# Four stacked graph-attention layers on one core: three pair sums kept in SBUF, and more steps for roots, source scores and turned rows

## The chip, the cores and the metric

The kernel runs on 1 core of one Trainium2 chip. The metric is the device time of one execution in microseconds. Engines are named as in the profile: PE is TensorE (matmul) and PEld its weight loads, DVE is VectorE, ACT is ScalarE, POOL is GpSimd, SP is SyncE, which here issues nearly all DMAs.

## The reference

A graph of N = 3327 nodes with 256 features each, a dense 0/1 adjacency matrix, and four attention layers, each followed by a residual sum and a layer norm. The last layer holds three attention steps of its own.

```python
def _L0(features, adj, Wq, Wk):                  # cosine attention
    att = where(adj > 0, Kn @ Qn.T, NEG); att = softmax(att, axis=1)
    prop = adj_mask * (att @ features) + (1 - adj_mask) * features
    return 0.5 * prop + 0.5 * features
def _L1(x, adj, W, a):                           # graph attention with leaky relu
    h = x @ W
    e = leaky_relu((h @ a[:D]) + (h @ a[D:]).T, 0.01)
    return elu(softmax(where(adj > 0, e, MASK_VAL), axis=1) @ h)
def _L2(x, adj, Wq, bq, Wk, bk, Wv, bv):         # dot-product attention
    q, k, v = x @ Wq.T + bq, x @ Wk.T + bk, x @ Wv.T + bv
    return elu(softmax(where(adj > 0, q @ k.T / sqrt(256), neg), axis=-1) @ v)
def _L3(x, adj, W0, W1, a1, W2, a2, W3, a3):     # x @ W0, then three steps like _L1
x = layernorm(x + _Li(x, adj, ...))              # for i = 0, 1, 2, 3
```

## The kernel before, in words

**Tiles and blocks.** The nodes are padded to 3328: NT = 26 tiles of 128 source nodes, and NB = 7 blocks of target nodes, six of 512 (4 tiles) and a last one of 256 (2 tiles). A pass (`Layer`, with keys 0, 1, 2, 3a, 3b, 3c) runs over the blocks b, and a block over the 26 steps j. A step makes one tile of attention weights (128 source nodes by 512 target nodes) and multiplies it into the values of these 128 nodes: the product goes to PSUM (`po`), where the block's sums gather.

**Weights.** In layers 0 and 2 PE makes scores (`ps`, L459 and L523), ACT takes the exponential (`ex`, L468 and L531), and DVE multiplies by the mask (`e`, L448). In layers 1, 3a, 3b and 3c ACT makes them from a row of source scores `u` and a column (`re`, L617), and DVE multiplies by the mask (`e`, L628). `make` runs LA = 2 steps ahead of the products.

**Products.** Most blocks multiply `e` straight into the values (L1282). Layer 2 and blocks 1 to 5 of layer 0 take two steps together in seven products instead of eight (`products`, L738). For this DVE adds and subtracts weights (`ssum`, L686 to L689), and four sums of the values of tiles 2p and 2p+1 are wanted (`tsums`, 128 x 513 floats for a pair p of 13). `combine` makes them once on DVE (L662 to L671) and writes them to DRAM (`t_d`, L672); `fetch_tsum` (L676) reads a pair back when a block comes to it. Tiles of the tag `tsum` have 3 buffers. For layer 0 `combine` is called in block 0, for pairs 0 to 12 at steps 9 to 21. In layer 2 the last pair's sums are used from SBUF in block 0 without a fetch.

**Adjacency.** In layer 0 each block's adjacency comes in 13 pieces of two tiles (`stage`, 512 KB, 3 buffers, L400). ACT turns a piece into a byte mask (L411, L412), and DVE adds it to a sum (`acc`, L416 and L420). At the end of a block `sum_adj` copies the sum (`af`, L431), and PE turns it (`pasum`, L435). The mask is written to DRAM (L890) for the later passes, which fetch it for a block (L385).

**Ends of blocks.** `finish` is a generator: it divides by the sums, applies the layer's weight, activation and norm, and stops at each `yield`. One part of it runs at each step of the next block (`advance`), and at j = 20 what is left is run at once. It holds: the copy of `po` (`p`, L916, or `y`, L872), which frees PSUM; `turn` (ACT copies `planes`, L793, a transposing DMA `turned`, L796, some steps of waiting, DVE copies, L803) for the rows before the projection (`pT`, then `pproj`, L947) and, in layer 1, for the normed rows (`ft`, then `pv`, L1032, then `combine` for layer 2); the dot products for the next pass's scores (`sd`, L551); after the last whole block, b = NB - 2 = 5, their greatest values and exponentials (`shift`, `keys`); and `rows`, where PE turns the source scores (`psr`, L595), ACT copies them (`srow`) and SP writes them (`s_d`). In the last block the mean row (`pmean`, L819) closes the values.

**Queries.** In layer 0 `queries0` prepares the next block's queries by such steps too: squares on ACT (L350), reciprocal roots on POOL (`rk`, L135 to L148), after some steps the scaling on ACT (`kr`, L366), the turning on PE (`pkT`, L370) and a copy on ACT (L371).

**Order.** Only the first four steps of the program stand in the order written. After that the tile framework's scheduler orders each engine's instructions from its own costs; the order in which the generators record them is what it starts from. [...] Tiles of one tag share a few buffers: `x4k` has two (for `xT`, `gT`, `y4`, layer 2's `tsum`, `planes`, `pT4`), PSUM's `pb` three, `po` five.

## Time and profile before

| what | value |
|---|---|
| runs of the kernel before | 2383.55, 2384.17, 2386.76 us (median 2384.17) |
| the profiled execution | 2385.32 us, of it 2383.5 us from the first to the last instruction |
| PE busy | 2349.8 us |
| PE's clock | 0.995 of full speed on average; 0.50 from 12.95 to 16.37 us and from 98.29 to 105.11 us |
| layer 0, block 0 | to 106 us |
| layer 0, blocks 1 to 6 | to 484 us |
| layer 1 | to 836 us |
| layer 2 | to 1408 us |
| passes 3a, 3b, 3c | to about 1727 us, 2047 us and the end |

The profile is of one execution. Times in it count from its first instruction. "Idle before" is the time an engine did nothing ahead of an instruction, with what ended it behind the arrow; in the chain, "issue" is time in which an engine waited for nothing that the profile shows. The ends of matmuls are modelled, so a wait of PE is best read from starts.

### The profile page before, as it was taken

Reading aid. Unit: us, or ns where it says so; the run is one execution under the profiler, and the core shown is the slowest. Engines: PE = TensorE matmul, PEld = TensorE weight load, DVE = VectorE, ACT = ScalarE, POOL = GpSimd, SP = SyncE. Lnnn points to the kernel's source line nnn. Section 1 sums busy time; section 2 is a strip of 40 time slices with the busy share of each in tenths; the row PEclk is TensorE's granted clock in tenths of the full one; section 3 lists DMA queues with packets and bytes.
Section 4 is the critical chain, followed back from the end, with each engine's and each line's share of the span. In section 5 each row is a group of like instructions: output and inputs, shape, how many; then the busy total and the mean of one; then the engine's idle time right before and its main releaser. Section 6 shows DMA issues by size and latency. Waiting matters only on the chain.

```text
span 2383.5 us, 33176 instructions
## 1 busy us (share of the span) xinstructions
PE 2349.8 (99%) x11965; PEld 1916.8 (80%) x11965; DVE 1609.4 (68%) x4318; ACT 1222.2 (51%) x1959; POOL 42.1 (2%) x168
## 2 busy tenths in 40 slices
PE   9999999999999999999999999999999999999997
PEld 6677787888888777667767798888888888888886
DVE  6779999966676657567567585556656555655665
ACT  4667776765555422222222255565655555655554
POOL 0000000000000000000000000000000000000000
PEclk9999999999999999999999999999999999999998
DMA  8555555523222322212212221221211111132120
GB/s 262 183 166 180 193 188 179 172 81 95 74 69 70 100 56 87 69 63 87 70 53 73 78 91 47 64 60 29 71 51 43 43 59 48 46 97 69 60 66 22
DMA packets 147720, 215.45 MB, mean 90 GB/s; under 512 B 76141, under 2 KB 101220, under 8 KB 142948
## 3 DMA queue, kind: packets, MB, share of 16 engines
q1 hardware_dynamic: 147284, 213.07, 28.9%
q8 instruction: 94, 1.54, 0.3%
q14 instruction: 70, 0.57, 0.1%
q10 hardware_dynamic: 272, 0.26, 0.0%
HBM read 168.32 MB, written 28.19 MB: 82 GB/s over the span
## 4 chain that ended last, share of the span: by engine, by line
PE 88%; DVE 7%; ACT 2%; DMA 2%; issue 1%; POOL 0%; POOLq 0%; SPq 0%; DVEq 0%; ACTq 0%
PE po L1282 48%; PE po L738 16%; PE ps L523 12%; PE ps L459 4%; PE pproj L947 3%; DVE e L448 1%; PE pv L1032 1%; PE pgq L482 1%; DVE acc L420 1%; DVE ejunk L551 1%; DMA turned<-planes 1%; PE po L1267 1%; ACT re L617 1%; DMA stage<-in_adj_a 1%; PE pq L305 1%
## 5 line engine op out<-in xcount | busy, mean ns | idle before, releaser
L1282 PE MATMUL po<-v,e 128*128 128x257 f32 x5616 | 1252.2, 381 | 1.9 <-ACT p L916 1.4
L1282 PEld LDWEIGHTS po<-v,e 128*128 128x128 f32 x5616 | 1063.2, 190 | 169.3 <-issue 10.9
L617 ACT ACTIVATE re<-u,nrh,th 128x512 f32<-128x512 f32 (+1 forms) x728 | 556.2, 780 | 478.4 <-DVE e L628 474.2
L628 DVE SCALAR_TENSOR_TENSOR e<-re,rh,mask 128x512 f32<-128x512 f32 (+1 forms) x702 | 502.5, 719 | 379.2 <-PE po L1282 355.8
L448 DVE SCALAR_TENSOR_TENSOR e<-ex,mask 128x512 f32<-128x512 f32 (+1 forms) x364 | 235.3, 649 | 198.9 <-ACT ex L531 157.8
L523 PE MATMUL ps<-gT,ft 128*128 128x512 f32 (+1 forms) x728 | 307.4, 563 | 0.0
L531 ACT ACTIVATE ex<-ps,off 128x512 f32<-128x512 f32 (+1 forms) x182 | 119.2, 656 | 359.9 <-PE ps L523 333.3
L738 PE MATMUL po<-tsums,ssum 128*128 128x128 f32 (+1 forms) x1794 | 250.9, 275 | 1.4 <-DVE ssum L688 1.2
L738 PEld LDWEIGHTS po<-tsums,ssum 128*128 128x128 f32 x1794 | 224.8, 192 | 3.3 <-DVE ssum L688 2.7
L523 PEld LDWEIGHTS ps<-gT,ft 128*128 128x128 f32 x728 | 132.1, 190 | 114.5 <-issue 111.7
L738 PEld LDWEIGHTS po<-v,e 128*128 128x128 f32 x1196 | 169.2, 191 | 68.0 <-issue 51.2
L738 PE MATMUL po<-v,e 128*128 128x129 f32 x1196 | 182.9, 275 | 1.9 <-DVE e L448 1.8
L468 ACT ACTIVATE ex<-ps,rq 128x512 f32<-128x512 f32 (+1 forms) x182 | 118.0, 653 | 115.9 <-PE ps L459 103.9
L459 PE MATMUL ps<-ft,ft 128*128 128x512 f32 (+1 forms) x312 | 143.4, 565 | 0.9 <-ACT ex L468 0.9
L420 DVE CUSTOM_DVE_ANT_0 acc<-acc,stage 128x1024 uint16<-128x1024 uint16 (+1 forms) x168 | 108.5, 646 | 14.7 <-DMA stage<-in_adj_a 10.9
L738 PE MATMUL po<-v,ssum 128*128 128x128 f32 x598 | 92.3, 275 | 0.0
L738 PE MATMUL po<-tsums,e 128*128 128x128 f32 x598 | 92.1, 275 | 0.0
L412 ACT ACTIVATE mask<-pos 128x1024 uint8<-128x1024 bf16 (+1 forms) x87 | 86.3, 992 | 2.0
L411 ACT ACTIVATE pos<-stage 128x1024 bf16<-128x1024 int32 (+1 forms) x87 | 85.6, 983 | 0.0
L947 PE MATMUL pproj<-w_l_w,pT 128*128 128x256 f32 x304 | 78.0, 381 | 3.5 <-DVE pT L803 3.5
L738 PEld LDWEIGHTS po<-v,ssum 128*128 128x128 f32 x598 | 79.4, 192 | 0.1
L738 PEld LDWEIGHTS po<-tsums,e 128*128 128x128 f32 x598 | 79.3, 192 | 0.0
(245 smaller groups left out, 1739.5 us busy)
## 6 DMA issues: line engine op xcount, KB each, us to landing
mask<-mask_d SPq DMA_DIRECT2D x30, 1664.0 KB
stage<-in_adj_a SPq DMA_DIRECT2D x78, 512.0 KB
tsums<-t_d SPq DMA_DIRECT2D x155, 256.5 KB
mask_d<-mask SPq DMA_DIRECT2D x6, 1664.0 KB
u<-s_d SPq DMA_DIRECT2D x24, 256.0 KB
xT<-in_xT SPq DMA_DIRECT2D x10, 512.0 KB
mask<-mask_d SPq DMA_DIRECT2D x5, 832.0 KB
t_d<-tsums SPq DMA_DIRECT2D x14, 256.5 KB
```

Source lines behind the costliest of these rows:

```text
L412: nc.scalar.activation(mask(b, j, 2), t_[:, : 2 * wd], AF.Sign)
L420: nc.vector.tensor_tensor(acc, acc, st[:, h * wd : (h + 1) * wd], ALU.add)
L448: nc.vector.scalar_tensor_tensor(e[:, :wd], t_[:, :wd], 0.0, mask(b, j), ALU.add, ALU.mult)
L459: nc.tensor.matmul(ps[:, :wd], FT[j // 4][:, 0, (j % 4) * P : (j % 4 + 1) * P], FT[b][:, 1, :wd], start=True, stop=True,)
L468: nc.scalar.activation(t_[:, :wd], ps[:, :wd], AF.Exp, scale=rq[:, j : j + 1])
L523: nc.tensor.matmul(ps[:, :wd], FT[j // 4][:, h, (j % 4) * P : (j % 4 + 1) * P], g[:, h, :wd], start=(h == 0), stop=(h == 1),)
L531: nc.scalar.activation(t_[:, :wd], ps[:, :wd], AF.Exp, bias=off, scale=1.0 / D**0.5)
L617: nc.scalar.activation(t_[:, :wd], self.u[b][:, :wd], AF.Relu, bias=self.nrh[:, j : j + 1], scale=self.th[:, j : j + 1],)
L628: nc.vector.scalar_tensor_tensor(e[:, :wd], t_[:, :wd], self.rh[:, j : j + 1], mask(b, j), ALU.add, ALU.mult,)
L738: nc.tensor.matmul(o, x, y, start=(p == 0 and g not in banks[:i]), stop=(p == NT // 2 - 1 and g not in banks[i + 1 :]),)
L947: nc.tensor.matmul(pm[:, :D], pT[:, h, :], w[L.w][:, h, :], start=(h == 0), stop=(h == 1),)
L1282: nc.tensor.matmul(pos[k], es[:, k * P : (k + 1) * P], V[L.i % 2][j], start=(j == 0), stop=(j == NT - 1),)
```

## The change

Five things change: which pair sums are fetched, and when some parts are recorded. What is computed stays the same.

1. The first three pairs' sums of layer 0 are kept for block 1: `combine` makes pairs 3 to 11 at steps 9 to 17, pair 12 at step 20 and pairs 0, 1, 2 at steps 21, 22, 23, and `make` doesn't fetch pairs 0 to 2 in block 1. They are still written to DRAM for the later blocks.
2. `queries0` waits 7 steps instead of 4 after the roots on POOL, except for block 1's queries.
3. After layer 0's last whole block two more steps stand ahead of `rows`.
4. `turn` waits longer for `pT` in the last block (5 steps in layer 1, 6 in 3a and 3b, instead of 3) and after the last whole block of 3a, 3b and 3c (6 instead of 5), and for layer 1's normed rows after the last whole block (4 instead of 3).
5. The end of layer 1's last whole block may run over steps 0 to 25 of the next block instead of 0 to 20.

```diff
@@ queries0
-            for _ in range(4):
+            for _ in range(4 if g == 1 else 7):
                 yield
@@
+    kept = {("0", 0): 1, ("0", 1): 1, ("0", 2): 1, ("2", NT // 2 - 1): 0}
+
     def combine(key, p, v, e=None):
...
-        here = key == "2" and p == NT // 2 - 1
-        if here or key == "0":
+        if (key, p) in kept or key == "0":
             t = work.tile([P, 4 * H + 1], F32, tag="tsum", name="tsums", bufs=3)
         else:
             t = work.tile([P, 4 * H + 1], F32, tag="x4k", name="tsum", bufs=2)
-        if here:
-            tsums[0, p] = t
+        if (key, p) in kept:
+            tsums[kept[key, p], p] = t
@@ finish, the rows for pT
-                    5 if b == NB - 2 else 3,
+                    3 if b < NB - 2 else 5 if L.key == "1" else 6,
@@ finish, layer 1's normed rows
+                    4 if b == NB - 2 else 3,
@@ finish, ahead of rows, b == NB - 2
                 L.gat_next.keys(0, ts_[-1] + 1)
                 yield
+                if L.key == "0":
+                    yield
+                    yield
@@ make
-        if strassen(L, b) and j % 2 == 0 and (L.key, b, j) != ("2", 0, NT - 2):
+        if strassen(L, b) and j % 2 == 0 and kept.get((L.key, j // 2)) != b:
             fetch_tsum(L.key, b, j // 2)
@@ the steps
-        if first and 0 <= j - 9 < NT // 2:
-            combine("0", j - 9, V[0], es)
+        if first and 9 <= j < 18:
+            combine("0", j - 6, V[0], es)
+        elif first and 20 <= j < 24:
+            combine("0", (j - 21) % (NT // 2), V[0], es)
@@
-        if j == 20 and not end:
+        if j == (25 if L.key == "1" and b == NB - 1 else 20) and not end:
             while pending:
                 advance()
```

## The prediction

> **What bounds the kernel now.** I read the busy times of the page first, then the chain, then PE's own idle stretches in the trace, and last what ended each of them.

> ```profile
> PE 2349.8 (99%) x11965; PEld 1916.8 (80%) x11965; DVE 1609.4 (68%) x4318; ACT 1222.2 (51%) x1959; POOL 42.1 (2%) x168
> ...
> PE 88%; DVE 7%; ACT 2%; DMA 2%; issue 1%; POOL 0%; POOLq 0%; SPq 0%; DVEq 0%; ACTq 0%
> ```

> PE works 99% of the span, and the diff neither adds nor removes a matmul. So only PE's idle time, 33.7 us of 2383.5, and time at a lowered clock can change. Idle stretches over 0.15 us come to 20.2 us in 21 places. The largest is the end of block 0 of layer 0 (timeline, columns: start, length, engine and line, then in brackets the idle time before and what ended it):

> ```profile
> 92.87 0.32 SPq L676 DMA_DIRECT2D tsums<-t_d  x1
> 93.28 0.38 SPq L400 DMA_DIRECT2D stage<-in_adj_a  x1
> ...
> 97.90 1.42 DVE L420 CUSTOM_DVE_ANT_0 acc<-acc,stage 128x1024 uint16<-128x1024 uint16 x2 [3.24 <-DMA stage<-in_adj_a]
> 99.24 0.68 DVE L448 SCALAR_TENSOR_TENSOR e<-ex,mask 128x512 f32<-128x512 f32 x1
> 99.84 0.42 DVE L431 CAST af<-acc 128x512 f32<-128x512 int32 x1
> ...
> 100.40 1.08 PE L435 MATMUL pasum<-ident,af 128*128 128x128 f32 x4 [4.44 <-DVE af L431]
> ```

> The adjacency piece is issued only at 93.28, behind a fetch of pair sums; DVE waits 3.24 us for it, in order, ahead of the last weights and of af; PE stands 4.44 us. The table by windows shows a second price, the granted clock (last but two columns):

> ```profile
> 94.88:98.29 3.41, 1.08 (x5) 0.59 (x4) 0.39 (x1) 1.35 (x2) 0.00 (x0) 1.00 1.04 336
> 98.29:105.11 6.82, 4.71 (x11) 3.25 (x12) 4.09 (x10) 0.69 (x1) 0.00 (x0) 0.50 0.56 237
> 408.87:412.28 3.41, 1.57 (x6) 0.90 (x6) 2.90 (x12) 3.38 (x5) 0.00 (x0) 1.00 0.11 42
> ```

> After a window with PE busy 1.08 of 3.41 us (32%) the clock is 0.50 for 6.82 us, and 4.71 us of matmuls run in it: 2.35 us lost. A window with 46% busy (408.87) lost no clock. The other places that the diff aims at:

> ```profile
>   POOL rk L148: 22.3, 6
> ```

> (what the instructions on tile kr waited for: ACT stands 22.3 us for roots on POOL; the trace shows PE losing 3.1 us of it at 408 to 414 and 0.8 us at 141 to 147, nothing in the other blocks), and three pieces of the chain:

> ```profile
> 466.92 0.27 PE psr L595
> ...
> 822.74 1.37 DVE ft L803 x2
> ...
> 824.24 3.69 PE pv L1032 x16
> ...
> 1708.53 0.72 DVE pT L803
> ```

> PE stands 1.15 us before psr, 0.96 before pv (for turned rows), 0.57 at 1708.7 and 0.66 at 2028.4 for pT.

> [...]the piece at 93.28 had its buffer free since ACT's L411 ended at 89.14.

> **The change part by part.** A scheduler sets each engine's order from the recorded steps, so I compared the built orders of the two kernels, engine by engine; a part whose orders don't move can't act.

> *Kept pair sums.* Three fetches (L676) leave SP at the end of block 0. Sums of pairs 3 to 11 are now made at steps 9 to 17, pair 12 at 20, pairs 0 to 2 at 21 to 23; the 13 writes stay. DVE does the same 65 small operations; 5 of them with the roots between take about 2.1 us (86.4 to 88.4), without roots 1.4. New order on SP: piece, write, piece (1,0), write of 12, piece (1,2), writes of 0 and 1, piece (1,4), write of 2.
> Step by step, with old durations: piece (1,0) waited for the write at 80.08 and left at 80.50; its buffer was free at 78.5 (L411 of 77.44 plus 1.05), so it leaves 2 us earlier and DVE's 0.46 us wait for it goes. Piece (1,2) left at 86.34 behind a fetch; now at 83.55 (L411 ends 83.51), landing by about 88. DVE, with two sums fewer before it, does the first sum of (1,0) at 82.9, weights, pair 0 with roots (to 86.2), weights, pair 1 with roots (to 88.4), half of (1,2) to 89.0, the last operation of pair 1 at 89.3. That releases its write (89.35) and piece (1,4) at 89.75, against 93.28. From issue to DVE's start took 4.62 us (93.28 to 97.90) behind a transfer of the same size issued 0.4 us before it; I keep that: 94.4. From there to pasum is 2.50 us as before: 96.9 instead of 100.40, **3.5 us**. Pair 2's sums (1.4 us) go into DVE's wait. PE is done with v_24's first matmul at 95.3 (the 0.47 us wait at 93.1 is gone), so it stands 1.6 us: a window stays at least 53% busy, above the 46% that kept the clock: **2.35 us** more. Bounds: if (1,4) takes 5.8 us (as from 86.34 to 92.16) 2.3 us and no clock; if the wait vanishes 5.1 + 2.35. I take 5.85.
> Behind the later write on SP stand the mask's 1.66 MB (now about 92.7, before 93.72) and piece (1,6), first used after 103: free. Pair 3's fetch still waits for pair 0's buffer.

> *Roots, 3 more steps.* In the built order of ACT the waiting kr (L366) hasn't moved, only its consumers (pkT on PE, its copy on ACT) by some two pairs; POOL's order is unchanged. So the waits for POOL stay: 0. Cover: kr's copy is needed first by the next block, some 8 steps later. Bounds: +3.9 if ACT were late enough after all, -0.6 for the copy (0.58 us) between two ex.

> *Source scores, 2 steps in block 5 of layer 0.* psr moves from v_10 to behind v_14. DVE is next: the e for v_11 stands behind eight L551 and starts at 467.04, those for v_12 and v_13 follow, and the e for v_14 waits on POOL's am and starts at 469.96, so v_14 starts at 470.4 instead of 470.66; psr's 0.11 comes after. **0.15 us** of the 1.15, bounds 0 and 1.1. The source row's write moves behind two pieces on SP and is read in layer 1's block 5.

> *Layer 1's last whole block to 25 steps, 4 steps for its turned rows.* pv moves behind v_25 and two ps pairs: 8 ps at 0.43 and 6 po at 0.217, 4.7 us of work between, so ft (done 824.1) is no longer waited for. po of layer 2 starts at 834.7 instead of 835.94: **1.2 us**. Next in line: pair 10's write lands 3.7 us after its last sum (827.80 to 831.56 before), DVE stands for it until 835.5, pair 11's write lands at 840.6, ACT's planes wait for its buffer (before 836.85), then ex for the fifth and sixth tile at 841.9 and 842.6, turned rows at 845.1, e by 846.2, and L688, the sum that PE wants first, at 847.3; PE wants it at 848.9 (1.1 us into the third pair's products). It fits with 1.6 us of room; bounds +1.2 and -2.

> *More steps for pT.* In layers 3a and 3b, block 5, and in 3c at the end, the first pproj and pT stand where they stood; only the second to fourth pproj come later. The waits of 0.57, 0.66 and 1.76 us stay: 0. In the half blocks pproj moves 3 steps; no wait was there, and the mean row (pmean behind v_19 instead of v_16) has 6 steps of 1.74 us until v_25 against 0.4 for its copy[...]. The mask now precedes s_d on SP; s_d is used a layer later. At the handover of layers PE stood 0.82 and 0.59 us for ACT's p; p has as many re before it as it had: I take +0.1, bounds -0.5 and +1.4.

> Sum: 5.85 + 0.15 + 1.2 + 0.1 = 7.3 us. Against the profiled execution (2385.32, span 2383.5) that is 2378.0 and 2376.2; that execution is 1.15 us above the median 2384.17, for which I forecast **2377.0**.

> **Rivals.**
> 1. The clock still falls, [...]the piece lands 1 us later: 3.5 - 0.5 + 1.4 = 4.4 gained, 2379.8. For it: 53% against 46% is a thin margin known from one window.
> 2. The end of block 0 is bound by the transfers (DMA share 1.04 at 94.88), and the wait only moves: 1.4 gained, 2382.8. Against it: at 92 to 94 hardly any transfer ran, the queue waited for its head.
> 3. Slower: in layer 2's first block everything hangs on one free buffer, in a chain of two writes (pair 10, pair 11), planes and turned rows. Each us that a write takes beyond 3.7 makes the sums two later, of which 1.6 are covered. From 8.2 us a write ((7.3 + 1.6) / 2 + 3.7) the whole gain is gone; at 9 us the loss is 9.0, 1.7 net: 2385.9. For it: the next block's mask (1.66 MB, L385) is issued in the same stretch. Against it: it was in the same queue before (821.06), and both writes took 3.7.
> 4. Roots act after all, or p comes earlier: 3 more, 2374.0.

> **How the numbers follow.** Forecast 0.57, first rival 0.16, second 0.08, third 0.10, fourth 0.09. About 0.2% (4.8 us: below 2379.4, above 2388.9) can be told from no change. Faster: the forecast less 0.03 for its spread, the fourth, and half of the first: 0.71. Slower by that much: 0.06 of the third, where a write passes 10.6 us or both handovers of layers lose as well. The rest, 0.23, is within. Range 2373.5 to 2382.0: from the fourth rival to short of the second, with the bounds of buffer waits and landings (+-2) inside; outside lie the second, the third and a little of the fourth, 0.2.

> **What would show it.** Right: no L676 between the pieces before 110; a piece issued near 89.8; pasum near 97 with under 2 us before it; clock 1.00 from 16 to the end; no wait at pv; kr still waiting some 22 us for POOL with 408 to 414 as before; pT's waits as before; psr's wait turned into one for e. Wrong: clock 0.50 near 98, a wait over 1 us on po L738 between 838 and 855, or kr's wait gone.

## The result, and the profile after

The changed kernel takes 2379.78 us (median of 8 runs, 2376.0 to 2381.62), the kernel before 2385.24 us (8 runs, 2383.55 to 2388.22). The ratio is 0.9974 with a 95% interval of 0.9963 to 0.9985: 6.2 us faster, between 3.6 and 8.8. The forecast was 2377.0 with 2373.5 to 2382.0; the sign and the range hold, the median lies 2.8 us above the number. Ratios here and below are of undisturbed runs alone: one slow run of roots26 (3065.42 us) and one of the kernel before beside it (6411.51 us) don't count in them.

The profiled execution of the changed kernel took 2376.0 us, the shortest of the eight. Its page begins (busy times, then shares of the chain):

```profile
PE 2345.3 (99%) x11965; PEld 1913.6 (81%) x11965; DVE 1608.6 (68%) x4318; ACT 1221.7 (51%) x1959; POOL 42.0 (2%) x168
...
PE 89%; DVE 6%; ACT 2%; DMA 2%; issue 1%; POOL 0%; DVEq 0%; ACTq 0%; SPq 0%; POOLq 0%
```

As many matmuls, 4.5 us less of PE's busy time (pasum's four took 1.08 us at 0.50 before and 0.63 us at 1.00 now), a span of 2374.2 us. The end of block 0 in the timeline:

```profile
87.17 0.33 SPq L400 DMA_DIRECT2D stage<-in_adj_a  x1
...
89.23 0.32 SPq L673 DMA_DIRECT2D t_d<-tsums  x1
89.64 0.38 SPq L891 DMA_DIRECT2D mask_d<-mask  x1
...
91.50 1.42 DVE L420 CUSTOM_DVE_ANT_0 acc<-acc,stage 128x1024 uint16<-128x1024 uint16 x2 [1.70 <-DMA stage<-in_adj_a]
...
93.44 0.42 DVE L431 CAST af<-acc 128x512 f32<-128x512 int32 x1
...
94.01 0.63 PE L435 MATMUL pasum<-ident,af 128*128 128x128 f32 x4 [0.74 <-DVE af L431]
```

No fetch of pair sums (L677 now) stands between the writes; the piece goes out at 87.17 and pasum waits 0.74 us instead of 4.44. In the trace before, the recorded clock changes at steps of 3.41 us (from 6.13 us on its stretches last 6.83, 3.41, 81.92 and 6.83 us); such a step is called a window here. The one in which that wait lies (columns: us, length, PE, PEld, DVE, ACT, POOL busy, granted clock, DMA share, GB/s):

```profile
92.75:96.16 3.41, 2.67 (x13) 1.73 (x12) 2.14 (x6) 1.70 (x3) 0.00 (x0) 1.00 0.89 365
```

PE is busy 78% of it, and the clock stays at 1.00 from 4 us up to the last 12 us. The other places, first what tile kr waited for, then PE's timeline:

```profile
  POOL rk L148: 22.1, 6
```

```profile
458.50 1.35 PE L1287 MATMUL po<-v,e 128*128 128x257 f32 x5 [0.81 <-DVE e L448]
...
818.85 1.46 PE L1034 MATMUL pv<-w_l_wvt,ft 128*128 128x256 f32 x6
...
1699.13 1.13 PE L948 MATMUL pproj<-w,pT 128*128 128x256 f32 x4 [0.60 <-DVE pT L804]
...
2340.13 1.13 PE L948 MATMUL pproj<-w_l_w,pT 128*128 128x256 f32 x4 [1.40 <-DVE pT L804]
```

Roots are still waited for; psr's wait has become one for e; pv has none; the first pproj waits as before.

A ledger shows more than busy times do. Both kernels make the same products, so I took the start of the same product in both traces; where the difference changes, time was gained or lost. Gains in us:

| place | predicted | first execution | second (run after_again) |
|---|---|---|---|
| start to the first product | 0 | 2.07 | 2.10 |
| to block 1's first product (pair sums) | 5.85 | 6.64 | 3.10 |
| blocks 1 to 5 of layer 0 (roots) | 0 | 0.27 | -0.34 |
| layer 0 to 1 (psr) | 0.15 | 0.05 | 0.02 |
| layer 1 to 2 (pv) | 1.2 | 1.18 | 1.19 |
| handovers of passes (p) | 0.1 | 0.40 | 0.38 |
| pproj inside 3b and 3c | 0 | -1.43 | -1.38 |
| the end | 0 | 0.21 | 0.22 |

Without the start the first execution gains 7.3 us, as the sum said, the second 3.2. That the first meets the sum is in part luck: 0.8 us more than forecast at the pair sums, and 0.2 to 0.3 each at the roots, the handovers and the end, make up for the 1.4 lost at pproj. The two executions differ most in the row of the pair sums, by 3.5 us: pasum comes 1.85 us later in the second, as the piece lands later, and 1.68 us go with a lost clock window behind it. The 0.6 us between them in blocks 1 to 5 are not explained.

### The profile page after: what moved, and what is told of

The parts are those of the page before. It is cut to its first block, busy times and chain, and to the rows that moved or that the text cites. A ratio compares the mean times of both kernels' runs of the same rounds, so it can differ in the third digit from the quotient of the medians.

```text
span 2374.2 us, 33168 instructions
## 1 busy us (share of the span) xinstructions
PE 2345.3 (99%) x11965; PEld 1913.6 (81%) x11965; DVE 1608.6 (68%) x4318; ACT 1221.7 (51%) x1959; POOL 42.0 (2%) x168
## 4 chain that ended last, share of the span: by engine, by line
PE 89%; DVE 6%; ACT 2%; DMA 2%; issue 1%; POOL 0%; DVEq 0%; ACTq 0%; SPq 0%; POOLq 0%
PE po L1287 49%; PE po L739 17%; PE ps L523 12%; PE ps L459 4%; PE pproj L948 4%; DVE e L448 1%; PE pv L1034 1%; DMA turned<-planes 1%; PE pgq L482 1%; DVE acc L420 1%; PE po L1272 1%; DMA stage<-in_adj_a 1%; DVE ejunk L551 1%; PE pq L305 0%; DVE y L882 0%
## 5 line engine op out<-in xcount | busy, mean ns | idle before, releaser
L448 DVE SCALAR_TENSOR_TENSOR e<-ex,mask 128x512 f32<-128x512 f32 (+1 forms) x364 | 235.3, 649 | 197.1 <-ACT ex L531 158.2
L420 DVE CUSTOM_DVE_ANT_0 acc<-acc,stage 128x1024 uint16<-128x1024 uint16 (+1 forms) x168 | 108.7, 647 | 10.3 <-DMA stage<-in_adj_a 6.4
L411 ACT ACTIVATE pos<-stage 128x1024 bf16<-128x1024 int32 (+1 forms) x87 | 85.6, 983 | 1.5 <-DVE e L448 1.5
L948 PE MATMUL pproj<-w_l_w,pT 128*128 128x256 f32 x304 | 78.5, 381 | 4.3 <-DVE pT L804 4.3
```

The lines of the kernel that those rows point to most:

```text
L420: nc.vector.tensor_tensor(acc, acc, st[:, h * wd : (h + 1) * wd], ALU.add)
L448: nc.vector.scalar_tensor_tensor(e[:, :wd], t_[:, :wd], 0.0, mask(b, j), ALU.add, ALU.mult)
L948: nc.tensor.matmul(pm[:, :D], pT[:, h, :], w[L.w][:, h, :], start=(h == 0), stop=(h == 1),)
```

## The experiments

Theory: in block 0 the head of SP's queue, a fetch waiting for its buffer, held the adjacency piece back, and PE's wait for it also cost the clock. The rivals: the clock falls by chance; the transfers are the limit; the gain comes from the other parts. Each group of kernels was timed beside the kernel before on the same chip, and ratios are to that: 2387.67 us for kept_alone, kept_undone, fill and fetch_pool, 2388.21 for after_again, roots_dve2, roots_dve6 and fill2, 2388.35 for pt10 and roots_dve, 2386.91 for roots26 and best.

**The first part alone, and all but the first part.** kept_alone is the kernel before with `kept` and the new order of `combine`; kept_undone takes them back out of the changed kernel:

```diff
-    kept = {("0", 0): 1, ("0", 1): 1, ("0", 2): 1, ("2", NT // 2 - 1): 0}
...
-        if first and 9 <= j < 18:
-            combine("0", j - 6, V[0], es)
-        elif first and 20 <= j < 24:
-            combine("0", (j - 21) % (NT // 2), V[0], es)
+        if first and 0 <= j - 9 < NT // 2:
+            combine("0", j - 9, V[0], es)
```

> The kernel before with the first part of the change alone: pair sums 0 to 2 kept for block 1, pairs made in the new order. Theory (the end of block 0 was held by the head of SP's queue): pasum's wait under 2 us instead of 4.4, and no clock of 0.50 after it; 5.9 us gained of the kernel before, so 2379.4, and PE's waits at pv, for roots and for pT as before. Rival 1 (the clock falls by chance of its window): 3.0 to 4.4 us, about 2381.5, with 0.50 near 98 in the profile. Rival 2 (the gain comes from the other four parts): under 1.5 us, 2384.

> The changed kernel with its first part undone: the 13 fetches of block 1 and the old order of the pairs are back, the other four parts stay. Theory: pasum waits some 4.4 us again and the clock is 0.50 for one window after it; only 1.2 (layer 1's end), 0.15 (psr) and 0.1 (p) are left, 1.45 us, 2383.8. Rival 2: 5 us or more are left, 2380.

Measured: 2382.26 us (11 runs), 0.9979 (0.9970 to 0.9988), 5.0 us gained; and 2385.11 us (13 runs), 0.9994 (0.9986 to 1.0002), 1.4 us. In kept_alone pasum waits 1.52 us and the clock holds; in kept_undone it waits 4.84 us, then the clock is 0.50 for 6.83 us, while pv's wait is gone (1.22 us gained there). So the parts add (5.0 and 1.4 against 6.2 for both), and by the medians over three quarters of the gain is the first; the intervals are about 2 us wide to each side. That the other parts made the gain, 5 us or more without the first, is ruled out.

**The clock without the wait's end.** fill puts six idle matmuls ahead of pasum in the kernel before:

```diff
+        if b == 0:
+            pf = bank("fill")
+            for k in range(6):
+                nc.tensor.matmul(
+                    pf, FT[0][:, 0, :P], FT[0][:, 1, :], start=(k == 0), stop=(k == 5)
+                )
         pa = bank("pasum")
```

> The kernel before with six matmuls of 128x512 ahead of pasum in block 0, whose product nobody reads; they lie in PE's wait of 4.4 us, so the wait isn't shortened and only the clock can change. Theory (half of the gain at this place is the clock): about 3 us of the wait are filled, no 0.50 after 98, 2.35 us gained, 2382.9. Rival (the lowered clock there costs nothing, or falls whatever PE does): 0.50 stays or the time is the same, 2385.2; if pasum comes later behind them, up to 0.5 us slower.

Measured: 2389.07 us (21 runs), 1.0008 (1.0001 to 1.0014), 1.9 us *slower*. PE's timeline at the place:

```profile
94.13 5.31 PE L436 MATMUL fill<-ft 128*128 128x512 f32 x12
99.66 0.63 PE L441 MATMUL pasum<-ident,af 128*128 128x128 f32 x4 [0.21 <-DVE af L431]
```

The matmuls take 5.31 us, not 3. Counted from the first product, pasum comes at 81.81 us against 81.95 before, so the wait isn't shortened; the clock stays at 1.00, and block 1's first product comes at 88.27 against 90.29: 2.02 us gained there, 1.9 of them between pasum and that product, by the clock alone. It is lost later, 3.3 us at the first pproj of 3a's last block and behind it (the answer of the DMAs from 1706 to 1708, with packets, MB and share; then the timeline):

```profile
q8 instruction: 1, 0.02, 2.7%
```

```profile
1708.23 1.36 DVE L809 COPY pT<-turned 128x1024 uint16<-128x1024 uint16 x2 [2.31 <-DMA turned<-planes]
...
1709.64 1.86 PE L953 MATMUL pproj<-w,pT 128*128 128x256 f32 x5 [2.15 <-DVE pT L809]
```

One 16 KB packet of the instruction queue begins at 1706.15 and takes 0.88 us. All but two packets of the transposing DMA end by 1706.18, the last two at 1707.04; in the kernel before no such packet falls there and PE waits 0.57 us instead of 2.15. That wait costs a clock window too (0.50 from 1710.34). By the ledger 1.1 us more are lost at a pproj near 1513, and 3.2 at the handover from 3b to 3c, where PE waits 2.15 us for p instead of 0.59 and a second window is lost (0.50 from 2051.67); that loss has no explanation here. I thought of shifted PSUM buffers first:

> The kernel before with the six idle matmuls of the run fill, but written into pasum's own PSUM tile, so that no further PSUM buffer is taken and the later buffers stay as they were. Theory (half of the gain at the end of block 0 is the clock; fill lost its gain in pass 3a to the shifted buffers): no 0.50 near 98, 2.35 us gained there and kept to the end, 2.35 in all. Rival 1: as in fill, the gain is there at 107 and is gone after pass 3a, so the shifted buffers weren't the cause. Rival 2: the clock is worth nothing there, 0.

fill2 (the same matmuls written into pasum's own tile) took 2388.16 us (13 runs), 1.0002 (0.9994 to 1.0011). The 3.3 us near 1711 are lost again, again with an instruction packet (1706.55 to 1707.43) ahead of the last two packets, so buffers weren't the cause. At the place itself the piece landed later in this execution (pasum at 83.30) and 0.50 us were gained. Neither run shows the 2.35 us in its total; what shows the clock's price is the stretch from pasum to block 1's first product over all executions: 6.0 us where no window was lost (6.5 in the two fills, where one more product of 0.43 lies behind pasum), 7.71 where one was (four others and fetch_pool), 8.34 and 8.92 where two were.

**Another queue instead of kept sums.** fetch_pool keeps nothing, but POOL issues block 1's fetches of pairs 0 to 2:

```diff
-        nc.sync.dma_start(t, t_d[key][p])
+        q = nc.gpsimd if key == "0" and b == 1 and p < 3 else nc.sync
+        q.dma_start(t, t_d[key][p])
```

> The kernel before, with the fetches of pair sums 0 to 2 for block 1 issued by POOL instead of SP. Nothing is kept and the same bytes move, only SP's queue is free of the three waits. Theory (the head of SP's queue was the cause): the last piece of block 0 is issued before 91, pasum's wait falls below 2.5 us, no 0.50 after it, 4.5 to 6 us gained, 2380. Rival (transfers are the limit, and keeping the sums helped as there is less to move): pasum still waits over 3 us, at most 1.4 us gained, 2383.8.

Measured: 2384.44 us (13 runs), 0.9990 (0.9981 to 0.9998), 2.4 us. SP's queue and POOL's:

```profile
88.73 0.32 SPq L672 DMA_DIRECT2D t_d<-tsums  x1
89.65 0.33 SPq L400 DMA_DIRECT2D stage<-in_adj_a  x1
90.74 0.49 SPq L891 DMA_DIRECT2D mask_d<-mask  x1
```

```profile
91.11 0.55 POOL L677 DMA_DIRECT2D tsums<-t_d  x1 [1.97 <-DMA t_d<-tsums]
94.14 0.54 POOL L677 DMA_DIRECT2D tsums<-t_d  x1 [2.48 <-DVE e L448]
```

The fetches now wait on POOL, the piece goes out at 89.65 against 93.28, and pasum waits 2.23 us. With the same bytes, pasum is 2.7 us earlier: the queue's head was the cause, not the transfers. By the ledger 3.3 us were gained up to block 1's first product, with one clock window lost in place of two. Of these, 0.7 went again by the end of layer 0 and 0.7 at the handover from 3a to 3b (PE waits 1.51 us for p, before 0.82); why isn't known.

**The clock by chance.** The changed kernel again:

> The changed kernel once more, unaltered, beside the others of this call. Theory: pasum waits under 2 us and no 0.50 after it in this execution too, and the ratio to the kernel before stays near 0.9974 (6.2 us). Rival 1 (the clock falls by chance of its window): 0.50 near 92 to 99 in this execution, or a ratio above 0.9985.

Measured: 2380.41 us (6 runs), 0.9973 (0.9961 to 0.9984), 6.4 us, the same ratio; but in this execution pasum waits 2.35 us and the clock falls. By windows, this execution:

```profile
92.69:96.10 3.41, 1.06 (x7) 0.66 (x6) 2.33 (x4) 1.35 (x2) 0.00 (x0) 1.00 1.05 402
96.10:99.52 3.42, 3.42 (x10) 2.11 (x9) 1.43 (x4) 0.69 (x1) 0.00 (x0) 0.50 0.69 270
```

and of two later kernels whose block 0 also keeps the sums, roots_dve and then best:

```profile
92.66:96.07 3.41, 1.51 (x9) 0.90 (x8) 2.56 (x5) 1.12 (x2) 0.00 (x0) 1.00 1.03 395
```

```profile
95.43:98.84 3.41, 1.44 (x8) 0.85 (x7) 2.56 (x5) 0.96 (x1) 0.00 (x0) 1.00 1.00 403
98.84:102.26 3.42, 3.42 (x8) 2.38 (x8) 1.75 (x5) 0.69 (x1) 0.00 (x0) 0.50 0.43 173
```

31% busy lost the clock, 44% kept it, 42% lost it. In nine executions that keep the sums pasum waited 0.74, 1.52, 1.77, 1.83 and 1.90 us with the clock kept, and 1.98, 2.06, 2.21 and 2.35 us with it lost. So in these eight kernels the first rival happens in four of nine executions, by where the piece lands. For the changed kernel itself it is one of two: the ratio came back as expected, but the expectation of a clock kept in this execution failed.

**Roots.** Of the changed kernel, blocks 2 to 6, block 6 alone, blocks 1 to 6, or blocks 2 and 6 have their roots on DVE. For the first:

```diff
-            lengths(rk[:, :n], ss[:, :n], n, nc.gpsimd, "prs")
+            lengths(
+                rk[:, :n], ss[:, :n], n, *((nc.gpsimd, "prs") if g < 2 else (nc.vector, "rs"))
+            )
```

> The changed kernel with the roots of blocks 2 to 6 made by DVE instead of POOL. Theory (ACT stands for POOL's slow roots, and three more steps didn't help, as ACT's kr stayed where it was in its order): ACT's wait for roots falls from 22 us to about 7, PE's waits at 399 to 405 (1.10, 1.81, 0.34) and 132 to 138 (0.56, 0.54) fall to under 1 us together, 3 to 4 us gained of the changed kernel. Rival (DVE, which makes the sums that PE wants, is held up by 14 small operations a block): new waits for ssum or e in blocks 2 to 6, gain under 1 us.

> The changed kernel with the roots of block 6 alone made by DVE instead of POOL; the order on ACT and PE is that of the changed kernel. Theory: the wait of ACT near 392 to 398 falls from 5.7 us to under 2.5, PE's three waits at 399 to 405 (3.25 us) to under 1, 2.3 to 3.2 us gained of the changed kernel. Rival (those waits of PE come from ACT's load of masks and exponentials, not from roots): PE's waits there stay above 2 us, gain under 1.

> The changed kernel with all roots of blocks 1 to 6 made by DVE, those for block 1 in the end of block 0 too; PE's order is that of roots_dve2. Theory (block 0's end hangs on the last piece's landing, with DVE idle for it): as roots_dve2, pasum's wait under 2.4 us. Rival (block 0's end is bound by DVE, which makes the pair sums there): the 14 operations of 0.15 us push pasum 1 to 2 us later and the clock falls, 2 to 4 us slower than roots_dve2.

> The changed kernel with the roots of blocks 2 and 6 alone made by DVE, those of the other blocks by POOL as before. Theory (in roots_dve2 blocks 2 and 6 gained 1.7 and 2.7 us, while blocks 3, 4 and 5, where POOL's roots hid, each lost 0.7 us to a new wait of 0.56 for ssum): both gains without the three losses, 4.4 us gained of the changed kernel, no wait near 203, 270 and 337. Rival (the new waits come from the other order of ACT that holds in all blocks): 2.3 us as in roots_dve2.

Measured: roots_dve2 2376.77 us (5 runs), 0.9950 (0.9938 to 0.9963); roots_dve6 2378.80 (5 runs), 0.9960 (0.9948 to 0.9973); roots_dve 2374.99 (5 runs), 0.9946 (0.9933 to 0.9960); roots26 2374.72 (median of 6 runs), 0.9950 (0.9936 to 0.9963). The expectation of roots_dve6 is wrong on one point: ACT's order is not that of the changed kernel; kr moved behind four ex and two pieces in block 5, as the scheduler now takes the roots to be late. In roots_dve2, what kr waited for, and PE's timeline:

```profile
  POOL rk L148: 4.8, 1
```

```profile
203.53 1.16 PE L741 MATMUL po<-tsums,ssum 128*128 128x128 f32 x8 [0.56 <-DVE ssum L691]
...
403.09 0.49 PE L741 MATMUL po<-v,e 128*128 128x129 f32 x2 [0.58 <-DVE e L450]
```

One wait of ACT is left (block 1's roots, still on POOL). PE's waits at 399 to 405 fall from 3.25 us to 0.58, those at 132 to 138 are gone; by the ledger against the first execution of the changed kernel 3.0 and 1.8 us. In roots_dve6 the waits at block 6 fall to 0.58 too. But three new waits of 0.56 us for ssum come, in the blocks where POOL's roots had hidden: the rival is right in part. roots26 leaves these out and has none of them, as its theory said. Over blocks 1 to 6 roots_dve2 gains 2.3 us by the ledger, roots26 3.9 and roots_dve6 1.7 (3.0 at block 6, the rest lost elsewhere). By totals the two can't be told apart: in roots26's profile a clock window was lost at block 0's end, in that of roots_dve2 none. In roots_dve block 0's end is as before (pasum waits 1.90 us), so DVE isn't its bound.

**More steps for pT.** pt10 is roots_dve2 with 10 steps, best is roots26 with them:

```diff
-                    3 if b < NB - 2 else 5 if L.key == "1" else 6,
+                    3 if b < NB - 2 else 5 if L.key == "1" else 10 if b == NB - 2 else 6,
```

> The kernel of roots_dve2 with 10 steps instead of 6 ahead of pT after the last whole block of 3a, 3b and 3c. In the built order of PE the first pproj then stands behind both matmuls of v_10 and not between them, and psr half a step later. Theory (the waits of 0.6 us at the first pproj stay in the changed kernel because its first pproj wasn't moved): with the first pproj one to three matmuls of 0.43 us later the two waits of 0.6 and the 1.4 at the end go, up to 2.5 us gained of roots_dve2. Rival (the turned rows are the head of the chain to the next pass's source scores): the waits return at the handover of passes, on p, with 1 us or more, gain 0 or a loss.

> roots26 with the 10 steps ahead of pT of run pt10. Theory: both gains add, as they lie in other passes: 4.4 and 2.0 us, 6.4 of the changed kernel. Rival (as the transposing DMAs and the instruction fetches fall anew, one of the two gives its gain back): under 4.

Measured: pt10 2374.40 us (5 runs), 0.9946 (0.9934 to 0.9959); best 2372.20 us (5 runs), 0.9941 (0.9929 to 0.9954), the fastest of all kernels here. Against the changed kernel's 0.9974 and 0.9973 that is 7.6 to 7.9 us, and the intervals don't overlap; 6.4 were expected. What the 10 steps add can't be told by totals (0.9946 against 0.9950 for roots_dve2, 0.9941 against 0.9950 for roots26), only by the ledger. PE in pt10, at the end of 3a:

```profile
1696.83 6.45 PE L1289 MATMUL po<-v,e 128*128 128x257 f32 x29
...
1719.24 1.57 PE L1289 MATMUL po<-v,e 128*128 128x257 f32 x6 [0.83 <-DVE e L630]
```

The first pproj no longer waits, but at the handover 0.83 us replace 0.53: by the ledger 3a and 3b gain 0.3 us each, the end of 3c 1.7. Both sides of the expectation hold, each at its place.

## Why the prediction was right, and where it was off

- **Kept pair sums, 5.85 us.** Right, step by step. Counted from the first product, the piece (1,4) was forecast to leave at 71.3 us (89.75 less 18.45) and took 70.8 to 72.1; from issue to DVE 4.62 was taken, 4.33 to 5.08 measured; pasum 3.5 us earlier: 2.5 to 4.3. The clock was priced at 2.35 us; the stretch behind pasum says 2.3 (8.34 against 6.02).
- **The step that was off: "a window stays at least 53% busy", "above the 46% that kept the clock".** Already the trace before held a window that didn't fit this yardstick: from 9.54 to 12.95 us PE is busy 66% by the modelled ends, and the next one is at 0.50 (lines in the last section). The 1.6 us of waiting were a fair middle of 0.74 to 2.35, but the clock fell at 1.98, inside that scatter. I took one landing time for a fixed one and gave the first rival 0.16; it came in four of nine executions. Where it comes, 3.1 to 3.6 us are gained here and not 5.5 to 6.6. With half of the executions so, the mean lies about 1.2 us above the forecast; the kernel before, 1.07 us longer by the median of eight runs than by that of three, accounts for most of the rest. The median is nearly the first rival's number (2379.8), but that is no sign that each execution goes that way: it lies between executions with and without the lost window.
- **Roots, 0.** Right, and for the reason given: kr stayed in its place on ACT, which waits 22.1 us against 22.3. With the roots on DVE the wait goes, so steps alone weren't what held it; but kr's place on ACT moved together with the engine (seen in roots_dve6), so which of the two did it isn't told apart.
- **Source scores, 0.15.** Measured 0.05 and 0.02. Next in line was the e named, and v_14's first product came 0.27 and 0.24 us earlier, much as forecast (0.26); its other products came only 0.16 and 0.13 earlier, and psr's 0.11 comes off that.
- **Layer 1's end, 1.2.** Measured 1.18, 1.19 and 1.22 in three executions. No wait came in layer 2's first block; the third rival, the slower one, didn't happen, its 1.6 us of room was enough.
- **pT, 0; p, 0.1.** The first pproj waits 0.60, 0.57 and 1.40 us against 0.57, 0.66 and 1.76. The handovers gave 0.4.
- **Not foreseen:** 1.4 us lost at pproj in blocks that the change doesn't touch, at turned rows that came later than before: PE waits 0.45 us at 1873.32 and 0.61 at 2095.83, where it didn't wait before. Each of the transposing DMAs there had an instruction packet inside (4.31 and 5.03 us from issue to the last packet; before, 3.80 without one and 4.44 with one). A smaller loss at the same place in 3c is in kept_alone (0.5) and fetch_pool (0.25) too, so it doesn't hang on one of these edits.
- **The second rival** (bound by transfers) fell with fetch_pool; **the fourth** (roots act) with the wait for kr.

## What to carry to other kernels

In the kernel before, the adjacency piece's buffer was free at 89.14 and the piece was issued at 93.28, right behind a fetch; with the fetches on POOL's queue it went out at 89.65. When a transfer is issued that long after its buffer came free, look at what stands ahead of it in its queue and what that waits for, then take it away or move it to another queue. When a wait on PE is near the length behind which the clock fell (1.98 us here, and not yet 1.90), forecast a spread and not a middle, since the landing of one transfer decided over 2 us in the cases above (1.7 us for the window, the rest for the landing itself). A step count in a generator moves only what the scheduler hadn't already put elsewhere; compare the built orders, and when nothing moves, change the engine or the buffer instead.

## What the runs showed of the hardware that was not expected

```profile
9.54:12.95 3.41, 2.25 (x15) 1.58 (x14) 2.02 (x11) 1.99 (x5) 0.00 (x0) 1.00 1.04 384
12.95:16.37 3.42, 3.42 (x6) 1.43 (x5) 2.72 (x14) 1.04 (x3) 0.00 (x0) 0.50 0.70 249
```

Of those 2.25 us, 0.91 are eight matmuls of one column each (pn, L317). PE's waits and these matmuls together make 2.06 to 2.08 us in the seven lost windows at the start and 1.89 to 1.98 in the seven kept ones, near the 1.98 and 1.90 us of block 0's end. Whether they count as waiting was not shown; no run tested it.

- **The windows begin at another time in each execution, and the start pays for it.** The first record of the full clock begins at 3.92 to 7.17 us (6.13 before, 4.01 in the first execution of the changed kernel). Where it began between 4.65 and 6.85 us (seven of fourteen executions) the window behind the one that holds PE's wait of 1.16 us for ft (L313, near 10 us) was at 0.50; at 3.92 to 4.08 and 7.09 to 7.17 it wasn't; there a part of the wait or of pn fell into another window. The first product of block 0 comes at 16.34 to 18.87 us (18.45 before, 16.38 in that execution), 2.5 us that no edit made.
- **Transposing DMAs with an instruction packet inside often took longer.** In the fourteen traces 378 transposing DMAs of 2080 packets had no other data beside them. From issue to the last packet the 313 without an instruction packet in that stretch took 3.78 to 3.87 us. Of the 65 with one, 47 took 4.08 to 5.13; the other 18 took 3.79 to 3.89, so a packet doesn't always cost something (in sixteen of these it began within 0.65 us of the issue, or before it). In the changed kernel the one issued at 2187.13, without such a packet, took 3.81 us, and the one issued at 2088.77, with a packet that began 3.02 us after the issue, 5.03 (answer of the DMAs from 2088.7 to 2094):

```profile
GB/s 0 0 0 0 0 0 0 0 0 19 166 218 218 214 218 203 193 212 212 228 214 230 218 325 203 168 71 14 0 0 6 8 10 10 10 10 156 288 38 0
...
q8 instruction: 1, 0.02, 1.1%
```

The transfer nearly stands for 1.1 us (the stretch of 0 to 10 GB/s; a column is 0.13 us) and then ends. What the small packets wait for there isn't visible; that it is the instruction packet is inferred from the coincidence in these cases; no run moved a packet alone.
